# Moved operand parts, an attention interleaved across heads, one load fewer ahead of a gather, and mixer norms in halves

## The chip, the cores and the metric

The kernel runs on one core of a Trainium2 chip. The metric is the device time of one execution in microseconds (us). The core has a matrix engine (PE), a vector engine (DVE), an activation engine (ACT), a general engine (POOL) and a queue engine (SP) that issues most loads here. Each works through a queue of its own in order, and they wait for one another by semaphores.

## The reference

The reference is a graph network of four layers over N = 512 nodes of D = 768 features, with 8704 edges. Each layer adds to x a graph convolution (GNN) and a global mixer of the layer-normed x, and then a feed-forward network (FFN). Cut to the first layer's parts and the order of the rest:

```python
edge_index = jnp.stack([src, dst])
xn = _layernorm(x, axis=-1)
x = x + _L0_gnn_ref(xn, edge_index, ...) + _L0_mix_ref(xn[None], ...)[0]
x = x + _L0_ffn_ref(_layernorm(x, axis=-1)[None], ...)[0]
...
# the end of _L0_gnn_ref: attention over all nodes, 8 heads of 96
qkv = nodes @ Wqkv.T + bqkv
q, k, v = jnp.split(qkv, 3, axis=-1)
q = q.reshape(n, H, DH) * DH ** (-0.5)
scores = jnp.einsum('nhd,mhd->hnm', q, k)
probs = jax.nn.softmax(scores, axis=-1)
attn = jnp.einsum('hnm,mhd->nhd', probs, v).reshape(n, D)
return nodes + attn @ Wo.T + bo
# _L0_mix_ref: random features, phi = exp(q @ rf.T - |q|^2 / 2), then linear attention
# _L0_ffn_ref and _L2_ffn_ref: each node to the one expert (of 8) with the largest gate
```

The third layer's GNN has three rounds of a relational convolution (four relations and a root matrix), its mixer is a linear attention; the fourth layer's FFN has 16 experts.

## The kernel before

Features lie on partitions in 6 chunks of 128 (`KC`), or nodes do in 4 tiles of 128 (`NT`); `HW` is 384, half of D. The stages follow one another on PE: the edge counts and mix0 (0 to about 260 us), gnn0, attention0, the FFN f0 (842 to 975), mix1, gnn1, ffn1, mix2, gnn2 (to 2225), the FFN f2, mix3, gnn3 and ffn3 (2450 to the end).

A framework turns this program into one queue for each engine: it orders the instructions itself by their dependencies and the order of the calls (`issue_after` and hand-made dependencies pin some), and sets the waits. Tiles come from pools; a tile that takes the place of an older one waits for that one's last reader. `self.ps()` gives one of 8 banks of PSUM.

**Products of fp32 in three parts.** An fp32 matmul is recorded by the profile as two. Where a product is large the kernel makes fp32r matmuls of parts instead: `operands` (called `ops` in the profile) cuts each chunk of a transposed activation in a top part, a scaled rest and their difference (ACT's `cut` L1969 and L1988, DVE's or POOL's subtraction L1983, DVE's L1990), and `thirds` does the same for a slice of 128 columns of a weight (ACT L1969, DVE L2003 and L2004). `heads3` then makes 18 matmuls for each of three such slices, 12 into one bank and 6 into another; `heads`, which attention0 uses before the change, makes 6 fp32 matmuls for each slice.

Where the parts lie is set by the pools. `parts_of` asks for a slightly larger tile and takes the parts 16 elements into it:

```python
    def parts_of(self, pool, spare=16):
        return pool.tile([P, 3 * KC * N + spare], F32R, name="ops")[:, 16 : 16 + 3 * KC * N].rearrange(
            "p (i k n) -> p i k n", i=3, k=KC)
```

Only mix1 uses it (L1573). The parts of the first layer (pool `L0o`: mix0, `fm3` and gnn0) and of the third (pool `L2`: mix2 and gnn2) are plain tiles.

**Weights.** `w()` and `wk()` load a block of 1152 KB from SP's queue into one of 6 buffers, which `thirds` shares. `self.gate` and `self.before` hold one load back: of the loads after the gate was set, the one that comes once `before` others have been issued waits for the gate, an instruction on POOL. In `moe` the gate is the last of the four indirect gathers `yb` (L1416), which fetch each node's row from `f_back` in HBM, where ACT's queue has written the experts' results `y`; `before` is 4. The loads after f0 are for mix1. PE then multiplies `y` into its node rows (L1424), adds two tiles' gathered rows by `diag` (L1427), DVE adds the rest to x and takes its norms (L1437).

**mix0.** For each half of the heads (g = 0, 1): keys by `heads3`, queries by `heads3`, with `norms` (|k|^2/2 and |q|^2/2: Square on ACT, a cut, a subtraction, two matmuls L812 for each of four heads, then copies to row 96 of `qk`), then `keys` and `queries` (exponentials of the random features) and the sums. `norms(qk, 1)` runs as a whole behind the first slice of the queries; `norms(qk, 0)` behind `keys`. Between the keys and the queries of g = 0, `checked` closes the edge counts: it sums them (PE), makes `deg` (L650, L651), adds to the diagonal of `AT`, and tests them by a matmul over `check`, whose outcome `self.big` is read later by SP to choose between gnn0 and a slower way.

**attention0.** v by fp32 matmuls (`tm`); then for each half of the heads queries and keys by `heads`, and head by head: four score matmuls, each with a maximum (L1145, DVE), an exponential with its sum (L1146, ACT), a reciprocal and a scaling (L1147, L1148, DVE); two steps of `masks` (the neighbour masks of a later stage: L1480 on DVE, L1483 on PE, L1484 on ACT); the transposes of `pr` into `prT` and the product with v. Then the output projection with `wo`, which adds to x. `aT`, its input, is a tile of its own; `nodesT` lies in pool `L0k`, in a place that the FFN's `xn` (pool `L1n`) takes later. f0 begins with `norm1` of each tile (statistics L469, scaling L473), and the transposes and gate matmuls of `xn`.

Of the kernel before, what the change touches and what calls it, by code (L numbers as in the profile page):

```python
# [10 lines left out]
F32 = mybir.dt.float32  # L11
# [11 lines left out]
P = 128  # L23
# [174 lines left out]
class Net:  # L198
# [325 lines left out]
    def counts(self, AT, EFT, deg, tmp, ones, meanwhile, then):  # L524
# [118 lines left out]
        def checked():  # L643
# [8 lines left out]
            for t in range(NT):  # L652
                at = slice(t * P, (t + 1) * P)
                nc.vector.tensor_mul(tmp, self.ident, deg[:, at])
                nc.vector.tensor_add(AT[:, t, at], AT[:, t, at].bitcast(F32), tmp)
            p = self.ps()
# [116 lines left out]
    def mix0(self, xnT, checked, ops, v, bv):  # L773
# [3 lines left out]
        with ExitStack() as c:  # L777
# [25 lines left out]
            def norms(qk, s):  # L803
                p = self.ps()
                for h in range(4):
                    sq = two.tile([96, N], F32, name="sq")
                    part = two.tile([96, 2, N], F32R, name="part")
                    nc.scalar.activation(sq, qk[:96, s, h, :], AF.Square)
                    self.cut(part[:, 0], sq)
                    nc.vector.tensor_sub(part[:, 1], sq, part[:, 0].bitcast(F32))  # L810
                    for i in range(2):
                        nc.tensor.matmul(p, half[:, 96 - 32 * h : 224 - 32 * h], part[:, i], start=h + i == 0, stop=h + i == 4)  # L812
# [64 lines left out]
            for g in range(2):  # L877
                if g:
# [3 lines left out]
                            lambda i: next(left, None))  # L882
                if g == 0:
                    checked()
                self.heads3(d["m0_wqkv"][g, 0], ops, qk[:96, 0], sb[:, 3 * g : 3 * g + 3], scale,
                            lambda i: norms(qk, 1) if i == 0 else None)
                fks = [keys(qk, 0), keys(qk, 1)]
                norms(qk, 0)
# [231 lines left out]
    def attention0(self, nodesT, bv):  # L1120
        nc, tc, d = self.nc, self.tc, self.d
        ns = self.chunks(nodesT)
        with ExitStack() as c:
            att = c.enter_context(tc.tile_pool(name="g0_att", bufs=1))
            two = c.enter_context(tc.tile_pool(name="g0_two", bufs=2))
            with tc.issue_after(self.after):
# [3 lines left out]
            aT = att.tile([P, KC, N], F32, name="aT")  # L1130
            self.tm(d["g0_wqkv"], ns, lambda t, nb, p: self.copy(v[:, t, (nb - 4) * HW : (nb - 3) * HW], p),
                    bv, nbs=(4, 5), bias_at=2 * D)
            for g in range(2):
                qk = att.tile([96, 2, 4, N], F32, name="qk")
                for s, b, scale in ((0, "g0_bq", 96 ** -0.5), (1, "g0_bk", 1.0)):
                    self.heads(d["g0_wqkv"][2 * s + g, 0], ns, qk[:, s], b, g, scale)
                for h in range(4):
                    pr = two.tile([P, NT, N], F32, name="pr")
                    prT = two.tile([P, NT, N], F32, name="prT")
                    st = self.small.tile([P, NT, 2], F32, name="sm")  # L1140
                    for t in range(NT):
                        p = self.ps()
                        self.acc(p, [(qk[:, 0, h, t * P : (t + 1) * P], qk[:, 1, h, :])])
                        m, s = st[:, t, 0:1], st[:, t, 1:2]
                        nc.vector.tensor_reduce(m, p, AX.X, OP.max, negate=True)  # L1145
                        nc.scalar.activation(pr[:, t, :], p, AF.Exp, bias=m, accum_out=s)  # L1146
                        nc.vector.reciprocal(s, s)  # L1147
                        nc.vector.tensor_scalar(pr[:, t, :], pr[:, t, :], s, None, OP.mult)  # L1148
                    for _ in range(2):
                        next(masks)  # L1150
                    for m in range(NT):
                        p = self.ps()
                        for t in range(NT):
                            self.tr(p[:, t * P : (t + 1) * P], pr[:, t, m * P : (m + 1) * P])
                        self.copy(prT[:, m, :], p)
                    hh = g * 4 + h
                    p = self.ps()
                    self.acc(p[:96], [(v[:, m, hh * 96 : (hh + 1) * 96], prT[:, m, :]) for m in range(NT)])
                    if h < 3:
                        self.copy(aT[:96, 3 * g + h, :], p[:96])  # L1160
                    else:
                        for i in range(3):
                            self.copy(aT[96:, 3 * g + i, :], p[32 * i : 32 * i + 32])
# [1576 lines left out]
```

## Time and profile before

| | |
|---|---|
| median of 3 runs | 3681.76 us (3681.06 to 3689.63) |
| profiled execution | 3680.38 us |
| its span in the profile | 3678.6 us |
| mean granted clock of PE | 0.992 |
| PE busy | 3574.9 us |
| DVE, ACT, POOL busy | 1661.8, 941.0, 476.8 us |
| mix0, 82 to 260: PE busy | 167.1 of 178 us |
| gnn0, 260 to 622: PE busy | 362.0 of 362 us |
| attention0, 622 to 842: PE busy | 208.8 of 220 us |
| f0, 842 to 975: PE busy | 119.6 of 133 us |

The span is the time from the first to the last recorded instruction; the time of the execution has a little before and after it. A row of the timeline has a start, a length, the engine, the line, the operation with its output and inputs, and the number of instructions; in brackets stands how long the engine was idle before it and what released it. Matmuls overlap in the records, so the rate of a run of matmuls is read from start to start.

### The profile page before, as it was taken

To read this page: it belongs to the slowest core of one execution; us is meant where nothing else is said; L and a number is where in the kernel's file an instruction comes from. 1 tells how busy PE (TensorE), PEld (TensorE's weight loads), DVE (VectorE), ACT (ScalarE), POOL (GpSimd) and SP (SyncE) were. 2 spreads that over 40 slices of the span, in tenths; PEclk is the share of its full clock that TensorE was granted. 3 is DMA by queue.
4 is the path that set the end of the run, shared out by engine and by line. 5 is a ranking of instruction groups with operands and counts; after the bars stand their busy time and mean duration, and the time that the engine had idled before them with its cause. 6 is when DMAs were issued, how large, how long until landed. Compare 5 with 4: busy or idle time off the path is not lost.

```text
span 3678.6 us, 40252 instructions
## 1 busy us (share of the span) xinstructions
PE 3574.9 (97%) x15885; PEld 2190.5 (60%) x15885; DVE 1661.8 (45%) x3348; ACT 941.0 (26%) x1674; POOL 476.8 (13%) x522
## 2 busy tenths in 40 slices
PE   8999999999999999999999998999999999999998
PEld 6667666445586675567878785556444444444443
DVE  8647663443333562346776764377321221221211
ACT  3533331221342352122343332254000000000000
POOL 8211111002002010011122222211000000000000
PEclk9999999999999999999999998999999999999999
DMA  4213113217312221012121216514999999999998
GB/s 179 86 49 129 47 70 130 72 40 307 131 52 106 83 106 70 13 65 85 65 78 52 78 51 239 200 52 170 371 424 424 423 424 424 424 424 424 424 425 352
DMA packets 96700, 714.56 MB, mean 194 GB/s; under 512 B 11712, under 2 KB 11969, under 8 KB 26481
## 3 DMA queue, kind: packets, MB, share of 16 engines
q1 hardware_dynamic: 75744, 604.81, 40.8%
q0 software_dynamic: 16848, 95.99, 6.8%
q10 hardware_dynamic: 3904, 11.01, 0.8%
q8 instruction: 132, 2.16, 0.2%
q14 instruction: 72, 0.58, 0.0%
HBM read 689.22 MB, written 22.54 MB: 193 GB/s over the span
## 4 chain that ended last, share of the span: by engine, by line
PE 77%; DMA 15%; DVE 4%; issue 1%; ACT 1%; POOL 0%; POOLq 0%; DVEq 0%; SPq 0%; ACTq 0%
PE ps L385 48%; PE ps L2545 7%; PE ps L2065 7%; DMA w<-in_f_Wd_dram 5%; DMA w<-in_f_Wu_dram 5%; DMA w<-in_f_Wg_dram 4%; PE ps L2561 4%; PE ps L406 3%; PE ps L991 3%; PE ps L2516 2%; PE ps L1823 2%; PE ps L1804 1%; PE ps L611 1%; DVE pt L1533 1%; DVE e L1532 1%
## 5 line engine op out<-in xcount | busy, mean ns | idle before, releaser
L2545 PE MATMUL ps<-w,xg 128*64 128x384 f32 x3072 | 565.3, 489 | 6.5 <-DMA w<-in_f_Wu_dram 3.0
L2545 PEld LDWEIGHTS ps<-w,xg 128*64 128x64 f32 x3072 | 237.0, 137 | 293.7 <-issue 262.3
L385 PE MATMUL ps<-ops,w 128*128 128x512 f32 x1404 | 347.8, 396 | 0.0
L2561 PE MATMUL ps<-w,hT 128*64 128x384 f32 x1536 | 320.3, 490 | 3.7 <-DMA w<-in_f_Wd_dram 2.2
L385 PEld LDWEIGHTS ps<-ops,w 128*128 128x128 f32 x1404 | 263.4, 188 | 61.6 <-issue 0.7
L2065 PE MATMUL ps<-ops,w 128*128 128x512 f32 x1080 | 267.2, 398 | 0.7 <-DVE w L2003 0.5
L385 PE MATMUL ps<-w,xnT 128*128 128x384 f32 x756 | 250.1, 486 | 0.3 <-ACT xnT L284 0.2
L2548 ACT ACTIVATE h<-ps 128x384 f32<-128x384 f32 x64 | 31.4, 490 | 795.2 <-PE ps L2545 795.2
L2065 PEld LDWEIGHTS ps<-ops,w 128*128 128x128 f32 x1080 | 203.4, 189 | 51.1 <-DVE w L2003 1.0
L2561 PEld LDWEIGHTS ps<-w,hT 128*64 128x64 f32 x1536 | 132.5, 137 | 164.7 <-issue 141.0
L1969 ACT ACTIVATE w<-w 128x768 fp32r<-128x768 f32 x162 | 136.2, 845 | 343.9 <-PE ps L385 277.2
L478 DVE TENSOR_TENSOR x<-x,ps 128x384 f32<-128x384 f32 x232 | 127.0, 552 | 205.7 <-PE ps L385 196.4
L385 PEld LDWEIGHTS ps<-w,xnT 128*128 128x128 f32 x756 | 142.5, 190 | 98.7 <-issue 4.5
L2549 DVE TENSOR_TENSOR h<-h,ps 128x384 f32<-128x384 f32 x64 | 35.4, 553 | 354.7 <-PE ps L2545 346.1
L385 PE MATMUL ps<-w,hT 128*128 128x384 f32 x552 | 184.6, 490 | 2.1 <-ACTq L1409 1.4
L1983 POOL TENSOR_TENSOR low<-low,ops 128x512 f32<-128x512 f32 x90 | 118.1, 1312 | 433.4 <-ACT ops L1969 433.4
L2003 DVE TENSOR_TENSOR w<-w,w 128x768 fp32r<-128x768 f32 x162 | 155.8, 963 | 19.4 <-ACT w L1969 18.7
L2004 DVE SCALAR_TENSOR_TENSOR w<-w 128x768 fp32r<-128x768 f32 x162 | 159.4, 985 | 2.9
L385 PEld LDWEIGHTS ps<-w,hT 128*128 128x128 f32 x552 | 103.1, 190 | 79.6 <-ACT xbT L284 7.1
L1990 DVE TENSOR_TENSOR ops<-ops 128x512 fp32r<-128x512 f32 x138 | 127.0, 929 | 19.0 <-ACT ops L1988 17.3
L2516 PE MATMUL ps<-xnT,sw 128*128 128x512 f32 x288 | 135.4, 603 | 0.0
L385 PE MATMUL ps<-C,parts 128*128 128x512 f32 x576 | 132.8, 390 | 0.0
(575 smaller groups left out, 5111.6 us busy)
## 6 DMA issues: line engine op xcount, KB each, us to landing
w<-in_f_Wg_dram SPq DMA_DIRECT2D x128, 1152.0 KB, 22.2
w<-in_f_Wu_dram SPq DMA_DIRECT2D x128, 1152.0 KB, 22.2
w<-in_f_Wd_dram SPq DMA_DIRECT2D x128, 1152.0 KB, 22.2
w<-in_g_w_dram SPq DMA_DIRECT2D x54, 1152.0 KB, 5.1
w<-in_m_wqkv_dram SPq DMA_DIRECT2D x20, 1152.0 KB, 5.8
w<-in_g_t_dram SPq DMA_DIRECT2D x12, 1152.0 KB, 5.1
w<-in_m_wp_dram SPq DMA_DIRECT2D x11, 1152.0 KB, 5.0
ea<-in_attr_dram SPq DMA_DIRECT2D x17, 512.0 KB, 4.3
```

Of the source, the lines that this page charges most:

```text
L385: i = self.nc.tensor.matmul(out, a, b, start=n == 0, stop=n == len(pairs) - 1)
L406: return self.nc.tensor.transpose(out, in_, self.ident[:k, :k])
L478: self.nc.vector.tensor_add(xs, xs, p)
L1969: return self.nc.scalar.activation(top, x, AF.Copy, scale=CUT).ins
L1983: (engine or nc.gpsimd).tensor_sub(low, v, ops[:, 0, k, :].bitcast(F32))
L1990: nc.vector.tensor_sub(dif, top.bitcast(F32), x.bitcast(F32))
L2003: nc.vector.tensor_sub(low, w, top.bitcast(F32))
L2004: self.sliced_last = nc.vector.scalar_tensor_tensor(dif, low.bitcast(F32), -TIMES, top.bitcast(F32), OP.mult, OP.add).ins
L2065: nc.tensor.matmul(outs[o], w[:, i, k], ops[:, i, k, :], start=n == 0 and i + k == 0, stop=n == 4 and i + k == KC)
L2516: i = nc.tensor.matmul(p, w[:, k, :], xnT[:, k, :], start=k == 0, stop=k == KC - 1)
L2545: nc.tensor.matmul(p[a * 64 : a * 64 + 64, :HW], xg[:, k, a * CAP : (a + 1) * CAP], ws[b][a][:, k, :], start=k == 0, stop=k == KC - 1)
L2561: nc.tensor.matmul(po[nb][a * 64 : a * 64 + 64, :HW], hT[:, f * P + a * 64 : f * P + a * 64 + 64], wd[a][:, f, nb * HW : (nb + 1) * HW], s ...
```

## The change

Four things are changed.

1. The parts of the first and third layer come from `parts_of`, with 48 spare elements in pool `L0o`; attention0 gets parts of its own by `parts_of`.
2. attention0 makes the parts of `nodesT` (subtractions on DVE) and uses `heads3` with them, keys first. `score` and `result` are split: the transposes and product of a head are a generator that is advanced after each score of the next head, and, at the end of a half, beside the next half's projections. `prT` has one buffer instead of two. `aT` is now `nodesT` itself.
3. In `moe` of f0, `self.before` is 3 instead of 4: the held load is the one before the one that was held.
4. In mix0 `norms` is a generator in two halves, advanced beside the queries' projection (for the keys), and around the making of the keys' features (for the queries); `checked` has a `yield` ahead of its last step, so that its test stands behind the queries' projection of g = 0.

```diff
@@ -653,6 +653,7 @@
                 at = slice(t * P, (t + 1) * P)
                 nc.vector.tensor_mul(tmp, self.ident, deg[:, at])
                 nc.vector.tensor_add(AT[:, t, at], AT[:, t, at].bitcast(F32), tmp)
+            yield
             p = self.ps()
             self.acc(p[:, :5], [(self.ones, check)])
             nc.vector.tensor_scalar(bad, p[:, :5], 0.0, None, OP.not_equal)
@@ -801,15 +802,23 @@
                 nc.scalar.mul(half[:, at], self.ones[:96, : at.stop - at.start], u)
 
             def norms(qk, s):
-                p = self.ps()
-                for h in range(4):
+                p, parts = self.ps(), []
+
+                def made(h):
                     sq = two.tile([96, N], F32, name="sq")
-                    part = two.tile([96, 2, N], F32R, name="part")
+                    parts.append(two.tile([96, 2, N], F32R, name="part"))
                     nc.scalar.activation(sq, qk[:96, s, h, :], AF.Square)
-                    self.cut(part[:, 0], sq)
-                    nc.vector.tensor_sub(part[:, 1], sq, part[:, 0].bitcast(F32))
-                    for i in range(2):
-                        nc.tensor.matmul(p, half[:, 96 - 32 * h : 224 - 32 * h], part[:, i], start=h + i == 0, stop=h + i == 4)
+                    self.cut(parts[h][:, 0], sq)
+                    nc.vector.tensor_sub(parts[h][:, 1], sq, parts[h][:, 0].bitcast(F32))
+
+                for hs in ((0, 1), (2, 3)):
+                    for h in hs:
+                        made(h)
+                    yield
+                    for h in hs:
+                        for i in range(2):
+                            nc.tensor.matmul(p, half[:, 96 - 32 * h : 224 - 32 * h], parts[h][:, i], start=h + i == 0,
+                                             stop=h + i == 4)
                 for h in range(4):
                     self.copy(qk[96:97, s, h, :], p[32 * h : 32 * h + 1])
 
@@ -880,12 +889,18 @@
                 qk = one.tile([97, 2, 4, N], F32, name="qk")
                 self.heads3(d["m0_wqkv"][2 + g, 0], ops, qk[:96, 1], sb[:, KC + 3 * g : KC + 3 * g + 3], scale,
                             lambda i: next(left, None))
+                of_keys = norms(qk, 1)
                 if g == 0:
-                    checked()
+                    check = checked()
+                    next(check)
                 self.heads3(d["m0_wqkv"][g, 0], ops, qk[:96, 0], sb[:, 3 * g : 3 * g + 3], scale,
-                            lambda i: norms(qk, 1) if i == 0 else None)
+                            lambda i: next(of_keys, None))
+                next(check, None)
+                of_queries = norms(qk, 0)
+                next(of_queries)
+                next(of_queries)
                 fks = [keys(qk, 0), keys(qk, 1)]
-                norms(qk, 0)
+                next(of_queries, None)
                 fq = queries(qk, 0)
                 for h in range(4):
                     hh = g * 4 + h
@@ -1121,46 +1136,67 @@
         nc, tc, d = self.nc, self.tc, self.d
         ns = self.chunks(nodesT)
         with ExitStack() as c:
+            ops = self.parts_of(c.enter_context(tc.tile_pool(name="g0_ops", bufs=1)))
             att = c.enter_context(tc.tile_pool(name="g0_att", bufs=1))
             two = c.enter_context(tc.tile_pool(name="g0_two", bufs=2))
             with tc.issue_after(self.after):
                 self.padded(self.wq1, 1, 4)
             masks = self.masks(c.enter_context(tc.tile_pool(name="mk", bufs=2)))
             v = att.tile([P, NT, D], F32, name="v")
-            aT = att.tile([P, KC, N], F32, name="aT")
+            aT = nodesT
+            sb = att.tile([P, KC], F32, name="sb")
+            nc.vector.tensor_scalar(sb, self.col("g0_bq", 0, KC), 96 ** -0.5, None, OP.mult)
+            self.operands(ops, lambda k: (nodesT[:, k, :], self.rest(), None), nc.vector)
             self.tm(d["g0_wqkv"], ns, lambda t, nb, p: self.copy(v[:, t, (nb - 4) * HW : (nb - 3) * HW], p),
                     bv, nbs=(4, 5), bias_at=2 * D)
+
+            def score(qk, h, t, pr, st):
+                p = self.ps()
+                self.acc(p, [(qk[:, 0, h, t * P : (t + 1) * P], qk[:, 1, h, :])])
+                m, s = st[:, t, 0:1], st[:, t, 1:2]
+                nc.vector.tensor_reduce(m, p, AX.X, OP.max, negate=True)
+                nc.scalar.activation(pr[:, t, :], p, AF.Exp, bias=m, accum_out=s)
+                nc.vector.reciprocal(s, s)
+                nc.vector.tensor_scalar(pr[:, t, :], pr[:, t, :], s, None, OP.mult)
+
+            def result(hh, pr):
+                g, h = divmod(hh, 4)
+                prT = two.tile([P, NT, N], F32, name="prT", bufs=1)
+                for m in range(NT):
+                    if m % 2:
+                        next(masks)
+                    p = self.ps()
+                    for t in range(NT):
+                        self.tr(p[:, t * P : (t + 1) * P], pr[:, t, m * P : (m + 1) * P])
+                    self.copy(prT[:, m, :], p)
+                    yield
+                p = self.ps()
+                self.acc(p[:96], [(v[:, m, hh * 96 : (hh + 1) * 96], prT[:, m, :]) for m in range(NT)])
+                if h < 3:
+                    self.copy(aT[:96, 3 * g + h, :], p[:96])
+                else:
+                    for i in range(3):
+                        self.copy(aT[96:, 3 * g + i, :], p[32 * i : 32 * i + 32])
+
+            left = iter(())
             for g in range(2):
                 qk = att.tile([96, 2, 4, N], F32, name="qk")
-                for s, b, scale in ((0, "g0_bq", 96 ** -0.5), (1, "g0_bk", 1.0)):
-                    self.heads(d["g0_wqkv"][2 * s + g, 0], ns, qk[:, s], b, g, scale)
+                for s, bias, scale in ((1, self.col("g0_bk", 3 * g, 3), 1.0), (0, sb[:, 3 * g : 3 * g + 3], 96 ** -0.5)):
+                    def beside(i):
+                        for _ in range(2):
+                            next(left, None)
+                    self.heads3(d["g0_wqkv"][2 * s + g, 0], ops, qk[:, s], bias, scale, beside)
                 for h in range(4):
                     pr = two.tile([P, NT, N], F32, name="pr")
-                    prT = two.tile([P, NT, N], F32, name="prT")
                     st = self.small.tile([P, NT, 2], F32, name="sm")
                     for t in range(NT):
-                        p = self.ps()
-                        self.acc(p, [(qk[:, 0, h, t * P : (t + 1) * P], qk[:, 1, h, :])])
-                        m, s = st[:, t, 0:1], st[:, t, 1:2]
-                        nc.vector.tensor_reduce(m, p, AX.X, OP.max, negate=True)
-                        nc.scalar.activation(pr[:, t, :], p, AF.Exp, bias=m, accum_out=s)
-                        nc.vector.reciprocal(s, s)
-                        nc.vector.tensor_scalar(pr[:, t, :], pr[:, t, :], s, None, OP.mult)
-                    for _ in range(2):
-                        next(masks)
-                    for m in range(NT):
-                        p = self.ps()
-                        for t in range(NT):
-                            self.tr(p[:, t * P : (t + 1) * P], pr[:, t, m * P : (m + 1) * P])
-                        self.copy(prT[:, m, :], p)
-                    hh = g * 4 + h
-                    p = self.ps()
-                    self.acc(p[:96], [(v[:, m, hh * 96 : (hh + 1) * 96], prT[:, m, :]) for m in range(NT)])
-                    if h < 3:
-                        self.copy(aT[:96, 3 * g + h, :], p[:96])
-                    else:
-                        for i in range(3):
-                            self.copy(aT[96:, 3 * g + i, :], p[32 * i : 32 * i + 32])
+                        score(qk, h, t, pr, st)
+                        next(left, None)
+                    for _ in left:
+                        pass
+                    left = result(g * 4 + h, pr)
+            for _ in left:
+                pass
             self.tm(d["g0_wo"], self.chunks(aT), self.add_x, self.bias(d["g0_bo"]))
 
     def moe(self, f, act, xn, xnT, wg, bs=None, fill=None, later=None, known=False):
@@ -1416,7 +1452,7 @@
                 i = nc.gpsimd.indirect_dma_start(out=ys[t], out_offset=None, in_=back,
                                                  in_offset=bass.IndirectOffsetOnAxis(ap=slot[:, t : t + 1], axis=0))
 
-            self.gate, self.before = i.ins, 4
+            self.gate, self.before = i.ins, 3 if f == "f0" else 4
             y = second(NA - 1, hT, w2)
             halves = [(t, slice(nb * HW, (nb + 1) * HW)) for t in range(NT) for nb in range(2)]
             ps = [self.ps()[:, :HW] for _ in halves]
@@ -2663,7 +2699,7 @@
             right.close()
             v = ck.enter_context(tc.tile_pool(name="L0k", bufs=1, side="right")).tile([P, NT, 8, 97], F32, name="v")
             nodesT = v.rearrange("p t h d -> p (t h d)")[:, : KC * N].rearrange("p (f n) -> p f n", f=KC)
-            ops = c0.enter_context(tc.tile_pool(name="L0o", bufs=1, side="right")).tile([P, 3, KC, N], F32R, name="ops")
+            ops = net.parts_of(c0.enter_context(tc.tile_pool(name="L0o", bufs=1, side="right")), 48)
             net.mix0(xnT, checked, ops, v, bv[0])
             bv0 = net.bias(net.d["g0_bv"])
             slot = net.which
@@ -2697,7 +2733,7 @@
         net.ffn1()
     with tc.tile_pool(name="L2", bufs=1) as pool:
         xn, xnT = normed(pool)
-        ops = pool.tile([P, 3, KC, N], F32R, name="ops")
+        ops = net.parts_of(pool)
         if "mix2" in only:
             net.mix2(xnT, ops)
         if "gnn2" in only:
```

## The prediction

> **What bounds the kernel now.** I read the page first, then the stages, then the timeline of PE around every line that the diff touches, then DVE and POOL where PE is idle. The page:
>
> ```profile
> span 3678.6 us, 40252 instructions
> PE 3574.9 (97%) x15885; PEld 2190.5 (60%) x15885; DVE 1661.8 (45%) x3348; ACT 941.0 (26%) x1674; POOL 476.8 (13%) x522
> PE 77%; DMA 15%; DVE 4%; issue 1%; ACT 1%; POOL 0%; POOLq 0%; DVEq 0%; SPq 0%; ACTq 0%
> ```
>
> PE is busy for 97% of the span, so time is won in two ways only: make PE's instructions fewer or shorter, or take out one of the 104 us in which it idles. The stages by windows (start:end, length, PE's busy time):
>
> ```profile
> 82.00:260.00 178.00, 167.07 (x709) 119.02 (x708) 93.33 (x160) 86.55 (x143) 43.05 (x47) 0.96 0.20 75
> 622.00:842.00 220.00, 208.76 (x696) 106.79 (x695) 91.01 (x194) 50.24 (x111) 12.71 (x16) 1.00 0.24 88
> 842.00:975.00 133.00, 119.61 (x540) 69.25 (x538) 47.82 (x128) 33.27 (x72) 33.32 (x37) 0.97 0.74 280
> 1695.00:2225.00 530.00, 525.06 (x2285) 424.25 (x2283) 384.03 (x485) 192.38 (x296) 115.28 (x88) 1.00 0.20 71
> ```
>
> They are mix0, attention0 (with its v projection and wo), the f0 FFN and the third layer's mixer and GNN. In the first three PE idles 11 to 13 us each; in the last hardly, and DVE (384 of 530) and ACT have room there.
>
> **Address of the parts.** The same 128x512 fp32r matmul goes at two rates. PE's timeline, start, length, line, count (mix1; then gnn2, two neighbours; then gnn0, two neighbours):
>
> ```profile
> 1007.81 15.12 PE L385 MATMUL ps<-ops,w 128*128 128x512 f32 x66
> ...
> 1736.86 5.76 PE L2065 MATMUL ps<-ops,w 128*128 128x512 f32 x24
> 1742.46 2.96 PE L385 MATMUL ps<-ops,w 128*128 128x512 f32 x12
> ...
> 308.71 2.95 PE L991 MATMUL ps<-ops,w 128*128 128x512 f32 x12
> 311.50 1.56 PE L385 MATMUL ps<-ops,w 128*128 128x512 f32 x6
> ```
>
> One matmul lasts 0.39 by the page, so mix1 gives (15.12 - 0.39)/65 = 226.6 ns from start to start; gnn2 (1742.46 - 1736.86)/24 = 233.3; gnn0 (311.50 - 308.71)/12 = 232.5. None waits, and all have the same shape. mix1 is the one place where `parts_of` moves the parts by 16 elements (64 bytes) in their tile. The built program puts the three weight parts at multiples of 256 bytes; mix1's parts lie on such a multiple, L0o's 128 and L2's 192 bytes off one. The other two operand pairs agree: AT with parts in gnn0 (325.44 to 336.36 in 48, 227.5 ns) and C with parts in gnn2 (1725.97 to 1736.86 in 48, 226.9) have both operands at the same offset. After the change L0o's, L2's and attention0's parts all lie on the multiple. So I take 226.7 for all: L0 has 216 (mix0) + 108 (`fm3`) + 648 (gnn0) = 972 matmuls, 972 x 5.7 ns = 5.5; L2 has 108 + 1620 = 1728, x 6.6 ns = 11.4. Together **-16.9**, between 0 (the cause is another) and -17.5. DVE stays under PE in both stages: in L2 525 us of PE lose 11 and DVE has 384.
> [...]
>
> **attention0.** Before, it runs from 657.72 to 810.11, 152.4:
>
> ```profile
> 657.72 31.06 PE L385 MATMUL ps<-v,w 128*128 128x512 f32 x72
> 688.62 3.60 PE L385 MATMUL ps<-qk 96*128 96x512 f32 x8
> ...
> 703.86 0.61 PE L406 MATMUL ps<-ident,pr 128*128 128x128 f32 x4
> 704.97 1.31 PE L406 MATMUL ps<-ident,pr 128*128 128x128 f32 x8 [0.50 <-DVE pr L1148]
> 706.69 0.66 PE L406 MATMUL ps<-ident,pr 128*128 128x128 f32 x4 [0.41 <-DVE pr L1148]
> 707.70 3.67 PE L385 MATMUL ps<-prT,v 128*96 128x512 f32 x8 [0.35 <-ACT prT L284]
> ```
>
> The projections take 30.9 for each half, 61.8; `heads3` makes 4 x 54 of the fast kind: 216 x 226.7 ns = 49.0, **-12.8**. The other 90.6 are eight heads of 11.3, of which PE works 9.55 (scores 3.43, mask 0.45, transposes 2.2, prT by v 3.47, by starts) and idles 1.77, 14.2 in all: the transposes wait for the softmax of the same head, the product for the copies of the transposes. In the new order the transposes and the product of head h-1 stand between the scores of head h, so each wait has about 9 us of cover, and what sets a head is the longest engine: DVE reductions 4 x 0.69, reciprocals 4 x 0.16, scalings 4 x 0.49, copies and counts 1.9, together 7.3; ACT exponentials 4 x 0.88, mask, copies, 6.4; both under 9.55. Left are the first head of each half, which has less beside it, and one table load of 1.28: I take 2.5, between 0 and the old 14.2. So 49.0 + 76.4 + 2.5 = 127.9, **-24.5** (-12.8 to -27). What hides the rest: the parts of `nodesT` (ACT cuts, DVE subtractions, 6 x 0.68 twice) run beside the 32 us of v projection; the twelve `thirds` (ACT 0.85, DVE 0.96 + 0.99 each) beside PE's heads, where DVE has 2 us a head to spare in the first half, the K and Q of the second half among them; each weight load, now waiting for the last third of an earlier block since a third takes a buffer of the same pool, lands about 5 us after its issue and has a projection of 12 to spare. If that cover fails, each of the four blocks costs up to 5.1 + 2.8 = 7.9.
>
> **The new wait at f0's start.** `aT` is now `nodesT`, and f0's `xn` lies on it. So the writes of `xn` (L473) wait for the last wo matmul:
>
> ```profile
> 832.45 0.68 DVE L473 TENSOR_SCALAR xn<-x,mv,rs 128x768 f32<-128x768 f32 x1
> ...
> 842.60 0.55 DVE L478 TENSOR_TENSOR x<-x,ps 128x384 f32<-128x384 f32 x1
> ...
> 844.55 0.68 DVE L473 TENSOR_SCALAR xn<-x,mv,rs 128x768 f32<-128x768 f32 x1
> ```
>
> Three of these were written early, at 832, 836 and 840; now all three stand beside the add and statistics of the fourth, 3 x 0.68 on DVE's queue less the 0.2 to 0.3 of gaps there: **+1.8** (1.5 to 2.4), PE's transposes behind it. The load of f0's gate, also held, is issued then, lands some 5 us later, just ahead of the gate's matmul (846.40 + 1.8); were it later it would cost up to 3.
>
> **One load fewer ahead of the gather.** Weights of mix1 stream over the DMA engines while the last `y` is written and `yb` gathered. f0, then f2, where no such load is left:
>
> ```profile
> 964.40 5.35 PE L1427 MATMUL ps<-yb,diag 128*128 128x384 f32 x8 [5.89 <-DMA yb<-f_back,slot]
> ...
> 2352.80 2.85 PE L1427 MATMUL ps<-yb,diag 128*128 128x384 f32 x8 [0.98 <-DMA yb<-f_back,slot]
> ```
>
> From the issue of the last write to the gather it is 948.55 to 957.51 = 8.96 in f0, and 2341.13 to 2345.81 = 4.68 in f2: 4.3 to win. The held load (1152 KB) then lands some 8 us later, with 60 us to its use; its third on DVE (0.95, at 955.51 in the gap before) falls into the chain of x and norms that follows the gather and ends the stage. So **-3.7**, between 0 (the write is slow for another reason) and -5.5 (PE's clock, 0.77 and 0.55 in 960:965 and 965:970 after the long idle, against 1.00 in f2's 2350:2355).
>
> **mix0's norms and check.** PE idles here 2.12 (on `deg`), 1.27, 0.23 and 1.14 in the first half, 2.70 in the second, 7.5 in all. The queries' projection now stands beside the key norms and ahead of the check's second step, so the 2.12 goes; but behind the last projection the norms of the queries still go Square, cut, subtraction, matmul, copy, and ACT and DVE have weight thirds of 0.85 and 0.99 queued there. I take **-2** (0 to -5). `big` is ready some 14 us later, with 100 us to the branch that reads it; the weight load moved ahead of that read on SP's queue only starts sooner.
>
> **Sum.** -16.9 - 24.5 + 1.8 - 3.7 - 2 = -45.3. The profiled execution took 3680.38 (span 3678.6), 1.4 below the median 3681.76: 3635.1 for it, **3636.5** for the median. 0.3%, 11 us, is about what a measurement of this kernel can tell from no change.
>
> **Rivals.**
> *The address is not the cause* (something else in mix1 makes it fast): 16.9 fewer, and attention0's 216 matmuls at 232.5 cost 1.3 more: 3654.7. For it: mix1 is the only place with `parts_of` to learn from. Against: AT and C. 0.13. [...]
> *The interleaving hides nothing* (each head is still 11.3, as buffers of PSUM come free late: scores, transposes, mask and product now share eight): 11.7 more, 3648.2. 0.09.
> *Slower than before*: PE's queue is in order, and the new order puts a step of head h-1 behind each of the 32 score matmuls. If the chain of a score (0.69 + 0.88 + 0.16 + 0.49 = 2.2) stands bare behind each of them, 32 x 2.2 = 70 come on top: 3707. It decides from (3692.8 - 3636.5)/32 = 1.8 us a step on. Against it: the transposes read `pr` of the earlier head, done 9 us before. 0.03.
> *The loads starve the projections*: 4 x 7.9 = 31.6, with the first rival 3686, no change; alone 3668. 0.04.
> *The gather's wait is not contention*: 3640; it lies inside the forecast.
>
> **How the numbers follow.** The forecast has 0.71. Low end: all terms at their best, -17.5 - 27 + 1.5 - 5.5 - 5 = -53.5, 3628. High end: the address brings nothing and the gather or the norms neither, 3654.7 + 5.7 = 3660. This leaves out the slower case, the starved loads and little else. Faster by over 0.3% (under 3670.7) 0.93, same 0.04, slower 0.03.
>
> **What would show it.** Starts of `ps<-ops,w` 226.7 ns apart in gnn0, gnn2 and attention0 (first rival: 232 to 233); attention0's projections 12.2 each, a head 9.6, no wait on `pr` or `prT` over 0.5 but at a half's start; `xn`'s four writes all after the last wo matmul; f0's idle before L1427 near 1 to 2 and clock 1.00 behind it; idle in 82:260 5 instead of 7.5. I am wrong if attention0 is over 140 or the rates stay.

## The result, and the profile after

The changed kernel takes 3637.3 us (median of 4 runs, 3634.67 to 3640.06), against 3684.76 of the kernel before (4 runs); the ratio is 0.9872, with a 95% interval of 0.9857 to 0.9888. 3636.5 was forecast. The span of the profiled execution goes from 3678.6 to 3632.8, 45.8 less, where the sum said 45.3. The sum came out so well because errors in its terms cancelled, and in part by luck: when the changed kernel was profiled again its span was 3640.5, 38.1 less than before. The experiments show which terms were off.

Lines of the page come first, then the stages by windows (start:end, length, the busy time of PE, PEld, DVE, ACT and POOL, PE's granted clock; the rows are mix0, attention0, f0 and the third layer):

```profile
span 3632.8 us, 40488 instructions
PE 3537.0 (97%) x15952; PEld 2201.7 (61%) x15957; DVE 1691.1 (47%) x3385; ACT 965.0 (27%) x1710; POOL 477.2 (13%) x522
...
PE 80%; DMA 10%; DVE 6%; issue 2%; ACT 1%; POOL 0%; POOLq 0%; DVEq 0%; ACTq 0%; SPq 0%
```

```profile
82.00:254.00 172.00, 162.74 (x709) 118.13 (x709) 92.18 (x160) 85.68 (x141) 43.07 (x47) 0.99 0.21 78
...
610.00:806.00 196.00, 190.87 (x764) 119.28 (x764) 118.08 (x228) 73.72 (x147) 12.39 (x15) 0.99 0.24 89
806.00:939.00 133.00, 121.59 (x546) 70.86 (x545) 50.20 (x132) 34.02 (x75) 32.37 (x36) 0.98 0.76 286
1660.00:2189.00 529.00, 516.70 (x2298) 426.13 (x2297) 389.89 (x508) 197.16 (x304) 119.40 (x95) 0.99 0.20 73
```

PE's idle time falls from 11.2 to 5.1 us in attention0, where the chain of waits had been, from 13.4 to 11.4 in f0, and from 10.9 to 9.3 in mix0, where the clock also rises from 0.96 to 0.99. The other gains are in shorter matmuls. (The third layer's windows can't be compared for idle time: the one here takes in two waits, of 1.39 and 5.62, that come at 2225 and later in the kernel before.) The table has the same stretches cut at PE's first matmul of each stage, in us, in the two kernels and in the experiments that bear on them:

| stretch | before | changed | forecast of the difference | others |
|---|---|---|---|---|
| mix0 and fm3, first parts matmul to gnn0's first | 185.21 | 177.45 | -2 and -1.8 (rate) | same kernel again 181.62; old norms 184.35 |
| gnn0 to attention0's first projection | 357.77 | 355.01 | -3.7 | plain parts 357.63 |
| attention0 | 152.39 | 129.43 | -24.5 | one head at a time 145.81; fp32 135.88 |
| wo to f0's gate | 36.29 | 38.70 | +1.8 | xn elsewhere 36.30 |
| f0, last 12 matmuls of w by hT to mix1 | 26.44 | 21.70 | -3.7 | same kernel again 22.22; four loads 23.78 |
| third layer, mix2's first parts matmul to f2's gate | 612.95 | 602.56 | -11.4 | plain parts 612.83 |

PE's timeline in gnn2 and gnn0, to be set beside the rows of before:

```profile
1700.22 5.60 PE L2101 MATMUL ps<-ops,w 128*128 128x512 f32 x24
1705.66 2.92 PE L385 MATMUL ps<-ops,w 128*128 128x512 f32 x12
...
300.15 2.88 PE L1006 MATMUL ps<-ops,w 128*128 128x512 f32 x12
302.87 1.52 PE L385 MATMUL ps<-ops,w 128*128 128x512 f32 x6
```

(1705.66 - 1700.22)/24 = 226.7 ns, and 2.72/12 = 226.7: both stages have mix1's rate, from 233.3 and 232.5. In attention0:

```profile
646.44 24.79 PE L385 MATMUL ps<-ops,w 128*128 128x512 f32 x108
671.07 4.46 PE L385 MATMUL ps<-qk 96*128 96x512 f32 x10
677.38 0.30 PE L406 MATMUL ps<-ident,pr 128*128 128x128 f32 x1 [1.86 <-DVE sm L1159]
...
687.30 1.02 PE L385 MATMUL ps<-qk 96*128 96x512 f32 x2
...
696.39 1.02 PE L385 MATMUL ps<-qk 96*128 96x512 f32 x2
```

The first two of the four projections take 24.6; a head takes 696.39 - 687.30 = 9.09 with no wait in it. What waits are left stand at the first head of each half. At f0's start the gate waits for its own weights (POOL's load, then PE):

```profile
808.76 0.56 POOL L410 DMA_DIRECT2D f_wg_gate<-in_f_wg_dram  x1 [31.26 <-issue]
```

```profile
814.57 1.91 PE L393 MATMUL ps<-xnT,f_wg_gate 128*32 128x512 f32 x12 [1.16 <-DMA f_wg_gate<-in_f_wg_dram]
```

And f0's end, from the chain of waits, where the write of `y` took 8.01 before:

```profile
916.05 2.31 DMA f_back<-y
...
919.38 3.95 DMA yb<-f_back,slot
...
923.38 0.95 DVE w L2039
...
925.26 0.87 DVE w L2040
```

Two pieces of a weight's third on DVE (L2039, L2040) now lie in the chain; the forecast had counted one of them. The idle of 5.89 ahead of the diag matmuls is gone, and PE's clock is 1.00 behind them, until it is granted at half for 6.8 us from 933.5 on. Such a half-clock stretch, in which PE's clock is granted at 0.50, comes up in several experiments below.

### The profile page after: what moved, and what is told of

It is laid out like the page before. It is cut to its first block, busy times and chain, and to the rows that moved or that the text cites. A ratio compares the mean times of both kernels' runs of the same rounds, so it can differ in the third digit from the quotient of the medians.

```text
span 3632.8 us, 40488 instructions
## 1 busy us (share of the span) xinstructions
PE 3537.0 (97%) x15952; PEld 2201.7 (61%) x15957; DVE 1691.1 (47%) x3385; ACT 965.0 (27%) x1710; POOL 477.2 (13%) x522
## 4 chain that ended last, share of the span: by engine, by line
PE 80%; DMA 10%; DVE 6%; issue 2%; ACT 1%; POOL 0%; POOLq 0%; DVEq 0%; ACTq 0%; SPq 0%
PE ps L385 46%; PE ps L2581 10%; PE ps L2101 6%; PE ps L2597 5%; DMA w<-in_f_Wg_dram 3%; PE ps L406 3%; DMA w<-in_f_Wu_dram 3%; PE ps L2552 3%; DMA w<-in_f_Wd_dram 2%; PE ps L1006 2%; PE ps L1859 2%; PE ps L1840 1%; DVE w L2039 1%; PE ps L611 1%; DVE pt L1569 1%
## 5 line engine op out<-in xcount | busy, mean ns | idle before, releaser
L385 PE MATMUL ps<-ops,w 128*128 128x512 f32 x1620 | 391.0, 392 | 0.0
L385 PEld LDWEIGHTS ps<-ops,w 128*128 128x128 f32 x1620 | 303.1, 188 | 65.3 <-issue 1.9
L2101 PE MATMUL ps<-ops,w 128*128 128x512 f32 x1080 | 260.5, 392 | 1.2 <-DVE xn L2110 0.6
L2005 ACT ACTIVATE w<-w 128x768 fp32r<-128x768 f32 x174 | 146.1, 846 | 350.8 <-PE ps L385 276.6
L2101 PEld LDWEIGHTS ps<-ops,w 128*128 128x128 f32 x1080 | 203.2, 189 | 45.5 <-issue 1.2
L2039 DVE TENSOR_TENSOR w<-w,w 128x768 fp32r<-128x768 f32 x174 | 167.2, 963 | 28.8 <-ACT w L2005 25.4
L2040 DVE SCALAR_TENSOR_TENSOR w<-w 128x768 fp32r<-128x768 f32 x174 | 170.9, 985 | 3.0
```

The lines of the kernel that those rows point to most:

```text
L385: i = self.nc.tensor.matmul(out, a, b, start=n == 0, stop=n == len(pairs) - 1)
L2005: return self.nc.scalar.activation(top, x, AF.Copy, scale=CUT).ins
L2039: nc.vector.tensor_sub(low, w, top.bitcast(F32))
L2040: self.sliced_last = nc.vector.scalar_tensor_tensor(dif, low.bitcast(F32), -TIMES, top.bitcast(F32), OP.mult, OP.add).ins
L2101: nc.tensor.matmul(outs[o], w[:, i, k], ops[:, i, k, :], start=n == 0 and i + k == 0, stop=n == 4 and i + k == KC)
```

## The experiments

The theory is that the rate follows the address, that the interleaving takes the waits out of attention0, and that the write shares the DMA engines with a load. The rivals are those of the prediction. Twelve kernels ran: the changed kernel once more, and eleven with one edit or two to it. Six of them (other offsets, weights moved, one head at a time, fp32, four loads, the check in one step) ran only once, so that their stages are read and not their times.

**The address.** The parts as plain tiles:

```diff
-            ops = net.parts_of(c0.enter_context(tc.tile_pool(name="L0o", ...)), 48)
+            ops = c0.enter_context(tc.tile_pool(name="L0o", ...)).tile([P, 3, KC, N], F32R, name="ops")
...
-        ops = net.parts_of(pool)
+        ops = pool.tile([P, 3, KC, N], F32R, name="ops")
```

> The parts of the first and third layer are plain tiles again (128 and 192 bytes off a multiple of 256); attention0 keeps its moved parts. If the address sets the rate, the 128x512 fp32r matmuls of mix0, fm3 and gnn0 start 232.4 ns apart again and those of mix2 and gnn2 233.3, against 226.7 in the changed kernel, and the time grows by 13 to 17 us (the stages of the trace gave 3.0 in gnn0 and 9.5 in the third layer, and some 1.5 in mix0). If something else of the change made them fast, the rates stay at 226.7 and the time stays within 3 us.

The time is 3649.39 us (4 runs; ratio to before 0.9916, 0.9899 to 0.9932), 12.1 over the changed kernel's first result and 7.9 over its second (3641.54, below), so under the 13 to 17 that were expected. The rates are 232.4 and 233.3 again; gnn0 grows by 2.6 and the third layer by 10.3. Then other offsets:

```diff
-    def parts_of(self, pool, spare=16):
+    def parts_of(self, pool, spare=16, at=16):   # the parts begin at element `at`
...
L0o: spare 48, at=32    g0_ops: at=8    L2: spare 32, at=24    m1_ops: as it was
```

> The changed kernel with the parts at other offsets: 64 bytes off a multiple of 256 in the first layer, 224 in attention0, 32 in the third layer, 0 in mix1 as before. The weight parts stay on multiples of 256. If only a multiple of 256 (or the same offset as the weights) is fast, mix1 alone shows 226.7 ns and the other three show 232 to 234. If what matters is to be off 128 or 192, or a coarser unit of 64, the first layer (64) is fast too. If the address is not the cause, all four show 226.7.

mix1 has 227 ns, attention0 (offset 224) 233.3 and the third layer (32) 233.3, as expected. The first layer (64) has 229.0 in `fm3` and gnn0, neither the one nor the other; in mix0 one run of 54 matmuls, from 187.03 on, went at 233.3, which stays open. Whether a multiple of 256 counts or the offset between the two operands, the next kernel told apart:

```diff
-        self.edge = edge.tile([P, 120], F32, name="edge")
+        self.edge = edge.tile([P, 128], F32, name="edge")     # 32 bytes, which move the weight buffers
...
L0o: spare 40, at=8    L2: at=8    g0_ops, m1_ops: as they were
```

> All weight buffers lie 32 bytes lower, so the weight parts are 224 bytes off a multiple of 256. The parts of the first and the third layer are put at 224 too, those of attention0 and mix1 stay at 0. If it is the offset between the two operands that counts, the first and third layer stay at 226.7 ns and attention0 and mix1 become slow, 232 to 234. If it is the offset of the streamed parts alone (a multiple of 256 is fast), it is the other way round: attention0 and mix1 at 226.7, the first and third layer slow. If 32 bytes are too few to count, all four stay at 226.7.

It is the offset between them. PE's timeline, mix1 and then gnn0:

```profile
1029.62 5.76 PE L385 MATMUL ps<-ops,w 128*128 128x512 f32 x24
1035.22 3.61 PE L385 MATMUL ps<-rf,ext 128*128 128x256 f32 x16
...
301.07 2.88 PE L1006 MATMUL ps<-ops,w 128*128 128x512 f32 x12
303.79 1.52 PE L385 MATMUL ps<-ops,w 128*128 128x512 f32 x6
```

mix1, whose parts did not move, slows to 5.60/24 = 233.3 because the weights moved, and so does attention0 (233.3). The first layer, 224 bytes off a multiple of 256 like the weights, has 2.72/12 = 226.7, and the third layer has about 227. The first rival is refuted.

**attention0 by halves of its edit.** The interleaving alone undone, then the three parts:

```diff
-                    left = result(g * 4 + h, pr)
+                    for _ in result(g * 4 + h, pr):
+                        pass
```

> The changed kernel, but in attention0 the transposes and the product of a head follow right behind its own four scores, as before the change; the projections stay in three parts by heads3. If the interleaving hides the waits for the softmax and for the copies of the transposes, attention0 (129.4 us in the changed kernel) grows by 9 to 12, to 139 to 141, with idle rows on pr and prT in each head as before. The rival, that it hides nothing or that the softmax is hidden by the shared banks alone, has attention0 at 130 to 132.

```diff
-                    self.heads3(d["g0_wqkv"][2 * s + g, 0], ops, qk[:, s], bias, scale, beside)
+                    ...   # heads' loop: fp32 matmuls of nodesT, next(left) twice after each slice
...
-            aT = nodesT
+            aT = att.tile([P, KC, N], F32, name="aT")
```

> attention0 with the new order of scores and results, but projections by fp32 matmuls of nodesT (queries and keys 30.9 us for each half) and an aT of its own. Then attention0 is 152.4 - 11 = 141 to 142, against 129.4 in the changed kernel, since 4 x 54 matmuls of 226.7 ns take 12.8 less; and wo's first matmul to the gate's takes 36.3 us as in the kernel before, since xn waits for nothing. The rival has the projections of three parts held back by thirds or loads, and attention0 then is under 139 here.

attention0 takes 145.8 in the first kernel and 135.9 in the second, and both expectations miss. The interleaving is worth 16.4 (145.81 - 129.43) or 16.5 (152.39 - 135.88), not 9 to 12, and the three parts 6.5, not 12.8. In the second kernel wo to the gate is 36.30, as expected. Its 135.9 is under 139, where the rival had it: the three parts do bring a delay of their own. The matmuls of the projections did become 2 x 6.3 shorter. What took half of that shows in the first kernel, on ACT and then on PE:

```profile
672.76 1.57 ACT L2006 ACTIVATE w<-w 128x768 fp32r<-128x768 f32 x2 [0.68 <-DMA w<-in_g_wqkv_dram]
674.35 1.28 ACT L1158 ACT_TABLE_LOAD   x1
675.65 0.69 ACT L1158 ACTIVATE pr<-ps,sm 128x512 f32<-128x512 f32 x1
```

```profile
677.75 0.45 PE L406 MATMUL ps<-ident,pr 128*128 128x128 f32 x1 [3.00 <-DVE sm L1159]
```

The first exponential waits behind two cuts of the next half's weight thirds, which ACT's queue took first, and the table; PE then waits 3.00, against 0.91 in the kernel before. In the second half the waits at the first head are 2.01 and 1.78. The changed kernel has the same cuts ahead of its table load (ACT), and the kernel with fp32 projections, which has no such cuts, waits 0.51 at its first head (PE) and 1.0 in all of attention0, where the changed kernel idles 5.0:

```profile
672.39 1.58 ACT L2005 ACTIVATE w<-w 128x768 fp32r<-128x768 f32 x2 [0.39 <-DMA w<-in_g_wqkv_dram]
```

```profile
686.72 0.30 PE L406 MATMUL ps<-ident,pr 128*128 128x128 f32 x1 [0.51 <-DVE sm L1157]
```

In the second half of the changed kernel no cut stands ahead of the first head. There the first maximum starts on DVE only at 738.16, behind 1.40 us in which DVE puts the parts of the last queries together; that this makes all of the 3.1 us of waits there was not tested.

**xn in another pool.**

```diff
-        xn = right.tile([P, NT, D], F32, name="xn")
+        left = keep.enter_context(tc.tile_pool(name="L1x", bufs=1))
+        xn = left.tile([P, NT, D], F32, name="xn")
...
-        net.moe("f0", AF.Gelu, xn, xnT, net.gate_of(right, "f0_wg"), "f0_bs", fill=part)
+        net.moe("f0", AF.Gelu, xn, xnT, net.gate_of(left, "f0_wg"), "f0_bs", fill=part)
```

> The FFN's xn and its gate weights lie in a pool on the other side of the memory, where nothing of wo's matmuls is read, so that xn's first three writes and the gate's load wait for nothing new. If the sharing of nodesT costs what the trace showed from wo's first matmul to the gate's (36.29 us before, 38.70 after), the stretch goes back to 36.3 and the time falls by 2.4 us. The rival: the later stage has slack, and the routing that follows gives the 2.4 back, so that the time stays.

The stretch is 36.30: the wait costs 2.4. The time, 3637.77 (ratio 0.9876, 0.9859 to 0.9892), does not show it; its four runs alone reach from 3633.78 to 3640.82. The half-clock stretches differ too: 3.4 us in f0's routing, where the changed kernel's profile had none, 10.2 instead of 3.4 in mix0, and none instead of 6.8 at f0's end.

**Four loads ahead of the gather.**

```diff
-            self.gate, self.before = i.ins, 3 if f == "f0" else 4
+            self.gate, self.before = i.ins, 4
```

> The changed kernel with four loads ahead of the gather, as before. If the load shares the DMA engines with the last write of y, the write takes about 8 us again from its issue, PE is idle 5 to 6 us ahead of the diag matmuls, its clock is 0.5 to 0.8 behind that, and the stretch from the last second-layer matmuls of f0 (12 of w by hT) to mix1's first matmul is 26.5 us as before instead of 21.7. The rival (the write was slow for another reason, and the whole stage only moved) leaves it at 21 to 23.

```profile
932.36 4.32 PE L1463 MATMUL ps<-yb,diag 128*128 128x384 f32 x8 [3.29 <-DMA yb<-f_back,slot]
```

The result lies between the two. From the write's issue to the gather it is 7.2 us against 3.3 (8.96 before), PE waits 3.29, and the stretch is 23.78 against 21.70 and, in the same kernel again, 22.22 (21.0 to 22.2 in the twelve profiles with three loads). So the write does share the engines with the load: they are 0.92 busy for four microseconds behind the write's issue (919.8 to 923.8), where the changed kernel has one such microsecond, of 0.88 (917 to 918). But the stage wins only 1.6 to 2.8 from it. DVE's chain behind the gather ends the stage, and with three loads it has the two pieces of the weight's third in it (0.95 + 0.87), which with four run at 924.74 and 926.07, inside the wait. In the kernel before the engines fall idle 5.5 us behind the write's issue, as they do here, and yet the gather starts 1.7 later; that part stays open.

**The norms and the check.** All of mix0's edit undone, then the check alone:

```diff
-                of_keys = norms(qk, 1)
...
-                of_queries = norms(qk, 0)
...
+                            lambda i: norms(qk, 1) if i == 0 else None)
+                fks = [keys(qk, 0), keys(qk, 1)]
+                norms(qk, 0)
```

> The changed kernel with mix0's norms and check as before the change. By the forecast the time grows by 2 us; by the profile of the changed kernel, where mix0 took 6.4 us less than before beyond the faster rate, by 6. Between the two stands the clock: the kernel before had PE at half clock for 6.8 and 7.1 us behind the two stalls of the norms, the changed one once for 3.5. If half-clock stretches follow from the stalls' length, they come back here; if they are a matter of luck in each execution, mix0's idle grows by 2 to 4 us and the rest depends on the run.

```diff
-                    check = checked()
-                    next(check)
+                    checked()
...
-                next(check, None)
```

> The changed kernel with mix0's norms in halves, but the check of the counts in one step between keys and queries, as before. By the forecast the wait on deg (2.12 us ahead of the check's matmul) comes back and the rest of the norms' gain stays: the first half of mix0 grows by about 2 us, the second half stays. The rival, in which the halves of the norms alone carry the gain, shows no change over 0.5 us in the first half.

With the old norms the time is 3647.2 (ratio 0.9905, 0.9889 to 0.9922). The interval overlaps that of the changed kernel's second result (0.9865 to 0.9898), so that the time alone does not show a loss. The stage mix0 is 184.35, near the 185.21 of before, with the same two half-clock stretches of 6.8 us at 153 and 218. (f0 had a half-clock stretch of 10.2 too, so not all of the time is the norms'.) With the check in one step the wait on `deg` is back, as expected:

```profile
129.64 0.36 PE L385 MATMUL ps<-edge,ones 128*128 128x5 f32 x2 [2.13 <-DVE deg L650]
```

The queries start 2.5 later; the first half of mix0, to its first matmul of `qk` by `rf`, grows by 3.3, of which a half-clock stretch behind the wait explains 1.7; from there to the same matmul of the second half it stays at 62.1. mix0 is 180.33 in this kernel, with 6.8 us of half clock, and 184.35 with the old norms, with 13.7. The 6.8 us more cost 3.4, so by these two profiles the halves of the norms themselves, without the check's move and without the clock, are worth only some 0.6.

**The same kernel again.**

> The changed kernel itself, for comparison on the same chip, and for what varies between executions: its instructions are the same, so every stage should repeat within 0.5 us except where PE ran at half clock. If the half-clock stretches are set by the stalls alone they come back at the same places with the same length (145: 3.4 us, 677: 3.4, 933: 6.8, 2182: 6.8, 2196: 17.1); if their place depends on the phase of a window of some 3.4 us, places come and go by whole windows, and the sum of the stage moves by 1.7 us for each.

The time is 3641.54 (4 runs; ratio 0.9881, 0.9865 to 0.9898). The stages of the table repeat within about 0.5 us but mix0, 181.62 against 177.45. Of the five half-clock stretches named, those of 677, 933 and 2196 come back with the same length, that of 145 does not (mix0 has one of 3.4 at 153 and one of 6.8 at 211 instead), and that of 2182 is 10.2 long. PE's timeline of the changed kernel and of the repeat at the same instructions, then the windows around them (PE's clock is the figure behind POOL's):

```profile
209.39 2.75 PE L385 MATMUL ps<-rf,qk 97*128 97x256 f32 x12
```

```profile
211.84 5.32 PE L385 MATMUL ps<-rf,qk 97*128 97x256 f32 x12
```

```profile
209.00:217.00 8.00, 6.91 (x25) 4.62 (x26) 4.27 (x6) 5.84 (x12) 7.72 (x6) 1.00 0.00 1
```

```profile
211.00:219.00 8.00, 7.33 (x17) 5.54 (x17) 4.58 (x5) 4.27 (x8) 7.72 (x6) 0.57 0.00 1
```

The same 12 matmuls take 2.75 or 5.32, behind the same waits of 0.36 and 1.13, so that the stalls alone do not set the places. By windows of 1 us, PE ran at half clock for 54.7 us between 100 and 2460 in the changed kernel, 68.2 in its repeat and 58.0 in the kernel before, always in pieces of 3.4 us or a multiple (6.8, 10.2, 17.1). Places that come and go by such pieces are what the second case of the expectation had; what sets them, a window or something else, no run shows. PE need not be idle throughout ahead of one: in the repeat it was busy for 1.9 of the 3.4 us ahead of the stretch at 211.3.

**Kept warm.** Matmuls are put into PE's waits in the routing of the third layer's FFN; a second kernel has `xn` elsewhere as well:

```diff
+            def warm(n):
+                p = net.ps()
+                for j in range((2, 4, 3)[n]):
+                    i = nc.tensor.matmul(p, net.ident, xnT[:, j, :], start=j == 0, stop=j == (1, 3, 2)[n])
+                return i.ins
...
+            net.moe("f2", ..., fill=warm, later=folded, known=True)
```

> The changed kernel with nine fp32 matmuls of 0.86 us, whose results nobody reads, put into PE's waits of the routing in the third layer's FFN (2, 4 and 3 of them, behind the logits, the counts and the places). In the changed kernel PE idles 1.63 and 3.76 us there and runs at half clock for 17.1 us from 2196 on, so that the transposes of xb take 1.54 instead of 0.8 and the first 12 matmuls of w by xbT 5.99 instead of 4.14. If the half clock follows from idle windows, it is granted whole again by 2205 and the stretch from the gate's matmuls to those 12 matmuls' end is 2 to 4 us shorter. The rival: the added matmuls delay the routing's own by as much, and the stretch stays or grows by up to 3.

The half clock of 17.1 us is gone (the granted clock is 1.00 in every window of 1 us from 2200 to 2290). PE's timeline, changed kernel and this one:

```profile
2209.77 5.99 PE L385 MATMUL ps<-w,xbT 128*128 128x384 f32 x12
```

```profile
2214.47 4.14 PE L385 MATMUL ps<-w,xbT 128*128 128x384 f32 x12
...
2221.41 4.25 PE L385 MATMUL ps<-w,xbT 128*128 128x384 f32 x12 [1.68 <-DVE xbT L282]
```

From the gate's first matmul to the end of these 12 it is 22.6 instead of 24.9, as expected; the next 12 then wait 1.68 for the copy of `xbT`, and at their start only 0.5 is left of 2.3. The time is 3641.41 (ratio 0.989, 0.9874 to 0.9907): no difference.

> The same nine matmuls, and the first FFN's xn and gate weights in a pool of their own. If both act alone, the time is 2.4 (wo to gate) and 2 to 4 us under that of the changed kernel, 0.1 to 0.2%, at the edge of what the rounds can tell; the stretches of the profile tell each of the two.

The time is 3635.44 (ratio 0.9864, 0.9847 to 0.988), 6.1 under the changed kernel on the same chip. It is the lowest of all, but the intervals overlap, so that it beats the changed kernel is not shown. wo to gate is 36.29. In f2 the wait of 1.68 is 0.25 here, and from the gate's first matmul to the first of `w` by `hT` it is 29.6 us, against 31.6 in the changed kernel and 31.2 in the kernel with the same nine matmuls alone. So the gain can last beyond the first 12 matmuls; why the copy came late in the one and not in the other stays open.

## Why the prediction was right

The total and its sign held, and so did the main mechanisms: the address, the interleaving, the wait of `xn` and the load beside the write. That it came within 1 us is luck: the sizes of the five terms were off by 0.6 to 4.0 us, in both directions, and the second result of the same kernel is 4.2 us from the first.

*Address.* The forecast was right in cause and rate. Its -16.9 was measured as 12.9 in two stages by undoing it, and 1.8 of mix0 to that by the rate: 14.7. Shorter matmuls met waits that the old rate had covered. In the third layer PE idles 12.4 us instead of 11.7, most of it a new wait of 0.58 for DVE at 1685; in gnn0 0.5 instead of 0.1, of it 0.27 for a cut on ACT at 328.72. The argument from AT with parts and C with parts, that equal offsets are fast, was the right reading; "a multiple of 256" was a special case of it.

*attention0.* -24.5 was forecast, -23.0 measured, and two errors cancel in it. The 9.55 of PE's work in a head was read from starts between waits and is 9.09, 3.7 too much over eight heads; so the waits to be hidden were larger than the 14.2 of the forecast, and the interleaving won 16.5. The term that was mis-sized the other way is the 2.5 of idle at the first heads: 129.4 - 49.0 - 72.7 = 7.7 is lost. Of it 5.0 is PE's idle time (1.86, 1.15, 1.09 and 0.90), about 1 the half clock at 677 (the kernel with four loads has none there and takes 128.4), and the rest was not followed. The forecast named the table load but not the two cuts ahead of it, although it placed the second half's thirds "beside" the heads: they lie ahead of them on ACT's queue.

*xn's wait.* It cost +2.4, against +1.8. The writes on DVE were priced a little high: the last six transposes of `xn` start 36.66 us behind wo's first matmul, 35.18 before, so 1.5 is theirs. The gate's load, put "just ahead" of its matmul, came late and made the other 0.9. The six transposes before, then in the changed kernel:

```profile
845.29 0.87 PE L406 MATMUL ps<-ident,xn 128*128 128x128 f32 x6 [0.76 <-DVE xn L473]
```

```profile
812.53 0.88 PE L406 MATMUL ps<-ident,xn 128*128 128x128 f32 x6 [1.01 <-DVE xn L473]
```

*The gather.* The stage is 4.7 shorter, against -3.7, but the load explains 1.6 to 2.8 of it; the rest of the difference to before, whose gather started 8.96 instead of 7.2 behind the write with the same four loads, stays open. The forecast's own figures, 4.3 to win less 0.95 on DVE, make 3.35, and DVE's part is 1.8.

*The norms.* mix0 fell by 6.0 beyond the rate in the profile and by 1.8 in the repeat, against -2. The idle that was counted, 7.5 at the places of the norms and the check, is 5.5 in the changed kernel, so this part was right, and nearly all of it is the check's (7.3 with the check in one step). The other part, which the forecast did not price here, is whether a half-clock stretch follows. The old norms had two of 6.8 us in both profiles that have them, the new ones between 3.4 and 10.2 us in all, over twelve profiles. The -6.0 of the one profile is luck: it had 3.4 us of half clock in mix0, the least of the twelve.

Of the rivals, none came about as it was priced: the softmax is hidden, the projections do not stand still for their loads, and PE is not held at each score. The three parts do bring a delay of their own, as the rival of the kernel with fp32 projections had it, but of some 6.3, a fifth of the 31.6 that starved projections would have cost.

## What to carry to other kernels

When the same matmul runs at two rates without waits in between, compare the addresses of its two operands before looking for a stall, and test by moving one of them. Before pricing what a first step waits for, read the other engine's queue ahead of it, the work for the next stage included. And before crediting an edit with a few us from one profile, look where PE ran at half clock, and take a second profile of the same kernel.

## What the runs showed of the hardware

In these kernels the start-to-start time of a 128x512 fp32r matmul went with the offset between the streamed and the weight operand's addresses, counted modulo 256 bytes: 226.7 ns at 0, 229.0 at 64 (but 233.3 in one run of 54), 232.4 at 128, 233.3 at 32, 192 and 224. With both operands at 224 it was 226.7 too (gnn0 with the weights moved), so that there the absolute address did not count.

The half-clock stretches of the kernel before, the changed one and its repeat lasted 3.4 us or a multiple (6.8, 10.2, 17.1), and they differed between two executions of one kernel: the same stage took 177.45 us with 3.4 of them in it, and 181.62 with 10.2.
